# A third set of one-hots and a second pick ahead of the transposed weights, in layers 1 and 2 of a graph network

## The chip, the cores and the metric

The kernel runs on one core of a Trainium2 chip. The metric is the device time of one execution in microseconds (us), lower is better. The engines are called as the profile calls them: PE (the matrix engine), PEld (its weight loads), DVE (vector engine), ACT (scalar engine), POOL and SP (which here issues most of the DMA transfers).

## The reference

Three graph layers over 6250 nodes of 64 features and 206,250 edges sorted by target node (100,000 random pairs in both directions, and a loop at every node). One layer, cut to what matters:

```python
q, k, v = x @ Wq + bq, x @ Wk + bk, x @ Wv + bv
e = edge_attr @ We
alpha = sum(q[dst] * (k[src] + e), -1) / sqrt(64)
p = exp(alpha - segment_max(alpha, dst)[dst])
w = p / segment_sum(p, dst)[dst]
out = segment_sum((v[src] + e) * w[:, None], dst) + x @ Ws + bs
```

Layers 0 and 1 end with a relu and a layer norm; behind the last come a log-softmax, a residual and a final layer norm.

## The kernel before

Edges go in chunks of 512, four chunks to a unit (L513): some 102 units. A layer is a loop over rounds, one unit a round, 99 of them (`for u in range(NU - 3)`, L1862). Everything is unrolled at build time, so each engine has one fixed queue of instructions, in the order in which the Python code emits them.

**Source rows.** The features of the source nodes come in part from gathers by POOL (L601, released one at a time by a small copy to a `gate` tile, L635) and in part from *picks* on PE. A pick takes rows out of a table of node features held in SBUF (`halves`) by multiplying with one-hot matrices. The class `Picker` (L1280) plans them: the nodes are cut into pairs of windows, 11 pairs in layers 1 and 2, and one job covers one pair for four rounds, with the jobs staggered. So in four rounds 11 jobs are due, three in each of three rounds and two in the fourth. A job takes these steps:

- `load` (L1298): SP loads the keys of its edges into a `key` tile (L1307), of which there are seven.
- `aim` (L1319): DVE compares the keys with row numbers and so writes four one-hot tiles `hot` (L1331). A set is the four tiles of a job. Two sets exist, from two pools taken in turn. At most two finished sets may be outstanding (the guard ahead of `pop`).
- `bank` (L1356): 24 matmuls (L1374) into a PSUM tile of tag "x"; ACT copies the result to `kept` (L1383, or L1386 for the last pair); then comes the `aim` of the next job that has none.

The tag "x" has two PSUM buffers, so a third bank writes over the first one's. [...]

**A round in layers 1 and 2** (L1868 to L1890), in the order of emission:

1. `store` (last round's sums go to DRAM) and `close_up`, which moves the finishing of ended node groups one step on: normalisation, exponentials, projections, spread over several rounds (L1480 on).
2. `scores`: PE multiplies (L1673, L1678), DVE takes the maximum of each row (L1685) and its negative (L1687), ACT takes the exponentials into `prob` (L1692).
3. `naturals`: PE transposes of the picked rows of the next unit (L1399, L1404), copied by DVE (L1400, L1406) and ACT (L1407, L1409).
4. `bank`: the first pick that is due.
5. `turn`: gates of the gathers, and PE transposes of the gathered rows (L1650) with two copies by ACT (L1653).
6. `ask` and `across`: SP loads for the next unit (L1598, L1612, L1629). In the code these stand between the two calls of `turn`.
7. `weights`: PE transposes of `prob` (L1704), copied by DVE to `probT` (L1707).
8. `bank` for every other pick that is due.
9. `sums`: 32 matmuls with `probT` as the weights (L1717), copied by ACT (L1725); copies of `settle` (L618); another `aim`, if the guard lets it.

So the order on PE in a round with three picks is scores, naturals, pick, turn, weights, pick, pick, sums. Layer 0 has a loop body of its own and its own rules for picks.

Of the kernel before, what the change touches and what calls it, by code (L numbers as in the profile page):

```python
# [11 lines left out]
BF16 = mybir.dt.bfloat16  # L12
# [7 lines left out]
P = 128  # L20
# [12 lines left out]
LB = 4  # L33
FB = 4
BW = 4
SL = 16
# [6 lines left out]
TURN = 4  # L43
# [399 lines left out]
def main_path(  # L443
# [80 lines left out]
    picks = ctx.enter_context(tc.tile_pool(name="picks", bufs=3))  # L524
# [755 lines left out]
    class Picker:  # L1280
# [38 lines left out]
        def aim(self):  # L1319

            self.load()
            if not self.aims or self.aims[0] not in self.keys or len(self.hots) > (self.layer > 0):
                return
            job = self.aims.pop(0)
            a, b = self.span(job)
            pool = later if self.layer and self.aimed % 2 else picks
            self.aimed += 1
            made = []
            for h in range(BW):
                hot = pool.tile([P, TURN * LB, 2, SL], BF16, name="hot", bufs=BW)  # L1330
                nc.vector.tensor_scalar(  # L1331
                    hot[:, a:b].rearrange("p k w e -> p (k w e)"),
                    self.keys[job][:, a * 2 * SL : b * 2 * SL],
                    rank[:, h : h + 1],
                    None,
                    ALU.is_equal,
                )
                made.append(hot)
            self.hots[job] = made
            del self.keys[job]  # L1340
            self.load()

        def due(self, k):

            if not self.jobs or self.jobs[0][0] > k:
                return False
            return self.layer > 0 or k >= U0 or self.jobs[0] in self.hots

# [444 lines left out]
    def move(n):  # L1793

        for _ in range(n):
            next(sorting, None)
            serve()
# [36 lines left out]
    def step(n=1):  # L1834
        for _ in range(n):
            advance()

    def close_up(n=1):
        step(n)
        for _ in range(n):  # L1840
            advance(ending)
# [4 lines left out]
    for layer in range(L):  # L1846
        line = Line(layer)
        def free(u, j):
            lead = 2 * LB if not layer else min(2 * LB, LB + u)
            release(layer, u * LB + j + 1 + lead, nc.scalar.copy)  # L1850

        def drip(u, n=1):
            points[0] += n
            lead = 2 * LB if not layer else min(2 * LB, LB + u)
            most = LB * (T - 1) if not layer else LB + 1
            release(layer, u * LB + min(points[0], most) * LB / most + lead, nc.scalar.copy)
            if not layer:
                next(first_ranks, None)

        if not layer:  # L1860
            picker = Picker(layer)
        for u in range(NU - 3):  # L1862
            close = u >= CLOSE
            this = chunks[layer, u]
            points = [0]
            line.store()
            if waiting:
                active.append(waiting.pop(0))  # L1868
            if layer:
                close_up()  # L1870
                line.scores(u)
                drip(u)
                picker.naturals(u + 1, "ma")
                picker.bank(u + 2)
                close_up(3) if close else step()
                this.turn(0, lambda: drip(u, 0.5))
                ask(layer, u + 1)
                chunks[layer, u + 1].across()
                this.turn(1, lambda: drip(u, 0.5))
                close_up() if close else step()  # L1880
                line.weights(u)
                close_up(3) if close else step()
                while picker.due(u + 2):
                    picker.bank(u + 2)
                drip(u)
                picker.load()
                line.sums(u)
                free(u, LB - 1)
                settle(layer, u + 1)
                picker.aim()  # L1890
                continue
            paces = (2,) * 4 if u < 2 else (2, 1, 1, 1) if u < U0 + 1 else (1,) * 4
            line.weights(u - 1)
            close_up()
            this.turn(0, lambda: drip(u))
            close_up(3) if close else step()
            move(paces[0])
            drip(u, 2)
            line.sums(u - 1)
            drip(u)  # L1900
            move(paces[1])
            line.scores(u, exps=False)
            picker.naturals(u + 1, "p")
            if picker.due(u + 2):
                picker.bank(u + 2, "g")
            picker.aim()
            drip(u)
            ask(layer, u + 1)
            chunks[layer, u + 1].across()
            close_up() if close else step()  # L1910
            this.turn(1, lambda: drip(u))
            if u:
                chunks[layer, u - 1].exps()
            drip(u)
            close_up(3) if close else step()
            move(paces[2])
            while picker.due(u + 2):
                picker.bank(u + 2, "g")
            drip(u)
            picker.load()  # L1920
            move(paces[3])
            free(u, LB - 1)
            picker.aim()

        more = layer + 1 < L
        for _ in sorting:
            pass
        serve()
        if not layer:
            first_layer.close()  # L1930
            later = ctx.enter_context(tc.tile_pool(name="later", bufs=1))
            halves[1] = later.tile([P, NB - EARLY, 2, D], F32, name="halves1")
            kept[1] = later.tile([P, TURN * LB, D], F32, name="kept1")
            nc.vector.memset(kept[1][D:, :, PART - D :], 0.0)
        assert not picker.jobs
        if more:
            picker = Picker(layer + 1)
            picker.aim()
        def early(n=1):
            halve(layer + 1, n)  # L1940
            if more and picker.ready(0):
                picker.bank(0, "s")

        u = NU - 3
        line.weights(u - 1)
        line.sums(u - 1)
        line.scores(u)
        ask(layer, u + 1)
        chunks[layer, u + 1].across()
        full, rest = chunks[layer, u], chunks[layer, u + 1]  # L1950
        line.store()
        full.turn(0)
        free(u, 0)
        free(u, 1)
        close_up()
        line.weights(u)
        early(3)
        close_up()
        full.turn(1)
        free(u, 2)  # L1960
        free(u, 3)
        assert not pending
        line.scores(u + 1, "x")
        early(3)
        ask(layer, u + 2)
        last = chunks[layer, u + 2]
        last.across()
        line.sums(u)
        line.store()
        close_up()  # L1970
        rest.turn(0)
        early(2)
        line.weights(u + 1)
        close_up()
        line.scores(u + 2, "x")
        early()
        line.sums(u + 1)
        line.store()
        close_up()
        last.turn(0)  # L1980
        early()
        line.weights(u + 2)
        line.scores(u + 3, "m")
        early()
        close_up()
        line.sums(u + 2)
        line.store()
        close_up()
        early()
        line.weights(u + 3)  # L1990
        line.sums(u + 3)
        line.store()
        close_up()
        early()
        if more:
            ask(layer + 1, 0)
            chunks[layer + 1, 0].across()
        while active or len(ending) > 1:
            close_up()
            early()  # L2000
        while ending and (not more or (layer, groups[-1][0]) not in written):
            close_up()
            early()
        if more:
            assert all((layer, g) in written for g, n in groups)
            for k in range(FB):
                if (layer + 1, k) not in loaded:
                    fetch(layer + 1, k)
                if k:
                    await_turn(layer + 1, k)  # L2010
                else:
                    gather_all(layer + 1, k)
            while ending:
                close_up()
            halve(layer + 1, len(groups))
            while picker.due(0):
                picker.bank(0)
            picker.naturals(0, "ma")
            settle(layer + 1, 0)
            while picker.due(1):  # L2020
                picker.bank(1)
            picker.aim()
# [45 lines left out]
```

## Time and profile before

| | us |
|---|---|
| median of 3 runs | 4270.91 |
| lowest and highest | 4266.38, 4275.15 |
| the profiled execution, its time | 4275.86 |
| the profiled execution, its span | 4274.1 |

Layer 0 with the planning takes to about 1950 us, the rounds of layer 1 lie between about 2071 and 3035 us, those of layer 2 between about 3165 and 4195 us; between them and behind the last come the changes of layer. In the lists of waits a line names the engine, the tile and line that waited, then the engine, tile and line that it waited for, and then the time in total, how often, and the longest. "issue" means that nothing in the trace explains the gap, "remote" a release by something other than an engine's instruction. In the timeline the columns are the start in us, the duration, the engine, the line, the operation, the tiles written and read with their shapes, and the number of instructions taken together (x24), whose duration is from the first one's start to the last one's end; in brackets stands the idle time before it and what ended it. In the table of windows each stretch has its length, the busy time of PE, PEld, DVE, ACT and POOL with the number of instructions, the granted PE clock as a share of full speed, the busy share of the DMA engines and GB/s.

### The profile page before, as it was taken

Reading aid. Unit: us, or ns where it says so; the run is one execution under the profiler, and the core shown is the slowest. Engines: PE = TensorE matmul, PEld = TensorE weight load, DVE = VectorE, ACT = ScalarE, POOL = GpSimd, SP = SyncE. Lnnn points to the kernel's source line nnn. Section 1 sums busy time; section 2 is a strip of 40 time slices with the busy share of each in tenths; the row PEclk is TensorE's granted clock in tenths of the full one; section 3 lists DMA queues with packets and bytes.
Section 4 is the critical chain, followed back from the end, with each engine's and each line's share of the span. In section 5 each row is a group of like instructions: output and inputs, shape, how many; then the busy total and the mean of one; then the engine's idle time right before and its main releaser. Section 6 shows DMA issues by size and latency. Waiting matters only on the chain.

```text
span 4274.1 us, 125157 instructions
## 1 busy us (share of the span) xinstructions
PE 3681.7 (86%) x44542; PEld 2464.7 (58%) x44542; DVE 2891.1 (68%) x9241; ACT 2394.9 (56%) x7113; POOL 2067.3 (48%) x1910
## 2 busy tenths in 40 slices
PE   4679998889999999987889999998778998888885
PEld 2345555555555655654666666666456666666663
DVE  5566888787788777774566666666456666666664
ACT  2334555555555555543566666666536676666664
POOL 4454554555455665552444444444415444444442
PEclk9789999999999999997999999999879999999997
DMA  5447787787777888874677777777647777777773
GB/s 119 101 131 188 201 213 203 192 211 200 206 198 211 226 212 209 218 196 131 146 183 189 192 185 186 188 193 182 152 96 191 177 181 184 187 186 179 176 187 83
DMA packets 828647, 768.02 MB, mean 180 GB/s; under 512 B 393233, under 2 KB 628903, under 8 KB 828014
## 3 DMA queue, kind: packets, MB, share of 16 engines
q1 hardware_dynamic: 673282, 571.05, 54.2%
q10 hardware_dynamic: 93932, 126.48, 8.4%
q0 software_dynamic: 60800, 62.38, 7.8%
q8 instruction: 356, 5.83, 0.6%
q14 instruction: 277, 2.27, 0.2%
HBM read 599.30 MB, written 160.27 MB: 178 GB/s over the span
## 4 chain that ended last, share of the span: by engine, by line


## 5 line engine op out<-in xcount | busy, mean ns | idle before, releaser
L601 POOL DMA_INDIRECT feat<-in_x,gate x860 | 1050.6, 1222 | 884.4 <-ACT gate L635 686.4
L1331 DVE TENSOR_SCALAR hot<-key,rank 128x512 bf16<-128x512 f16 (+3 forms) x3024 | 908.2, 350 | 372.5 <-PE ps_x L1374 167.5
L601 POOL DMA_INDIRECT feat<-x,gate x816 | 796.8, 976 | 745.3 <-ACT gate L635 479.1
L1374 PEld LDWEIGHTS <-halves 128*64 128x64 bf16 x18144 | 963.4, 113 | 285.7 <-issue 206.1
L1374 PE MATMUL ps_x<-hot,halves 128*64 128x256 bf16 (+1 forms) x13248 | 836.7, 276 | 41.6 <-issue 31.2
L1717 PE MATMUL ps_g<-feat,probT 128*32 128x128 f32 x9672 | 436.5, 283 | 92.4 <-issue 61.6
L1064 PE MATMUL ps_x<-hit,rest 128*64 128x512 bf16 (+3 forms) x3200 | 459.1, 359 | 6.0 <-issue 5.1
L1409 ACT COPY featT<-kept 64x512 f32<-64x512 f32 x584 | 361.5, 619 | 144.3 <-PE ps_g L1374 42.6
L1053 DVE TENSOR_SCALAR hit<-ruler,pos 128x512 bf16<-128x512 f16 (+3 forms) x1600 | 422.9, 334 | 1.7 <-PE ps_m L1078 1.4
L1717 PEld LDWEIGHTS ps_g<-feat,probT 128*32 128x32 f32 x9672 | 286.5, 112 | 221.5 <-issue 175.6
L1685 DVE TENSOR_REDUCE most<-ps_s 128x1 f32<-128x512 f32 x297 | 204.1, 687 | 300.6 <-PE ps_s L1678 111.9
L601 POOL DMA_INDIRECT few<-x,gate x198 | 193.6, 978 | 379.4 <-ACT gate L635 113.0
L1374 PE MATMUL ps_g<-hot,halves 128*64 128x256 bf16 (+2 forms) x4560 | 302.3, 281 | 74.1 <-ACT kept L1383 28.5
L1653 ACT COPY featT<-ps_a 64x512 f32<-64x512 f32 x584 | 338.6, 580 | 15.6 <-PE ps_a L1650 4.1
L1678 PE MATMUL ps_s<-featT,q 128*32 128x512 f32 x2376 | 333.7, 621 | 2.9 <-ACT featT L1653 1.3
L1064 PE MATMUL ps_x<-hit,raw 128*64 128x512 bf16 (+3 forms) x1600 | 311.0, 367 | 4.5 <-issue 4.1
L1383 ACT COPY kept<-ps_x 128x256 f32<-128x256 f32 (+2 forms) x502 | 185.1, 370 | 210.8 <-remote 128.6
L635 ACT COPY gate<-src_b 128x1 int32<-128x1 int32 x1762 | 289.9, 191 | 8.7 <-ACT keys L1136 1.4
L1692 ACT ACTIVATE prob<-ps_s,part 128x512 f32<-128x512 f32 x297 | 204.2, 688 | 161.0 <-issue 48.7
L1704 PE MATMUL ps_p<-ident,prob 128*128 128x128 f32 (+1 forms) x1224 | 199.1, 286 | 91.9 <-ACT prob L1692 89.8
L1064 PEld LDWEIGHTS <-rest 128*64 128x64 bf16 x3200 | 203.8, 113 | 116.6 <-issue 30.0
L1725 ACT COPY part<-ps_g 128x128 f32<-128x128 f32 (+1 forms) x309 | 82.2, 266 | 273.0 <-PE ps_g L1717 43.8
(261 smaller groups left out, 5162.4 us busy)
## 6 DMA issues: line engine op xcount, KB each, us to landing
feat<-eaP SPq DMA_DIRECT2D x292, 512.0 KB
featT<-eaS SPq DMA_DIRECT2D x292, 512.0 KB
key<-keyS SPq DMA_DIRECT2D x712, 128.0 KB
raw<-in_ea SPq DMA_DIRECT2D x200, 256.0 KB
eaS<-eT ACTq DMA_DIRECT2D x200, 256.0 KB
eaP<-eN ACTq DMA_DIRECT2D x200, 256.0 KB
to<-toS SPq DMA_DIRECT2D x292, 128.0 KB
part<-part SPq DMA_DIRECT2D x600, 32.5 KB
```

The source lines that it names most:

```text
L601: nc.gpsimd.indirect_dma_start(out=spares[layer, k] if c is None else loaded[layer, k][:, c, t, 0], out_offset=None, in_=xts[layer][:, :], ...
L635: copy(gate, index[:, i : i + 1])
L1053: nc.vector.tensor_scalar(hit, ruler[:, : REACH[t]], self.pos[:, at : at + 1], None, ALU.is_equal)
L1064: nc.tensor.matmul(self.px[i][j * D : (j + 1) * D, : REACH[t]], self.part(i, part)[:, (j * T + t) * D : (j * T + t + 1) * D], self.hits[t, ...
L1331: nc.vector.tensor_scalar(hot[:, a:b].rearrange("p k w e -> p (k w e)"), self.keys[job][:, a * 2 * SL : b * 2 * SL], rank[:, h : h + 1], None,
L1374: nc.tensor.matmul(px[w * D : (w + 1) * D, a:b], third(halves[block >= EARLY][:, at : at + 1], part)[:, 0], made[h][:, a:b, w], start=(h = ...
L1409: nc.scalar.copy(featT[:D, :, w * P : (w + 1) * P], kept[0][w * D : (w + 1) * D, at : at + LB])
L1653: nc.scalar.copy(self.featT[:D, :, at : at + P], pt[h * D : (h + 1) * D])
L1678: nc.tensor.matmul(self.p_s[rows], self.q[:, j * STRIDE : j * STRIDE + W], self.featT[:, j, :], start=False, stop=True)
L1685: nc.vector.tensor_reduce(top[:n], self.p_s[:n], AX.X, ALU.max)
L1692: nc.scalar.activation(self.prob[:n], self.p_s[:n], AF.Exp, bias=self.part[:n, P : P + 1], accum_out=self.part[:n, P + 1 : P + 2],)
L1717: nc.tensor.matmul(p_g[rows, :].rearrange("n (h d) -> n h d", h=2), self.probT[:, t, rows], batch[:, c + j, t], start=(t == 0), stop=(t == ...
```

## The change

The one-hots of layers 1 and 2 get a third set: of three jobs one takes the tiles of pool `picks` (four tiles, one set) and two take those of pool `later` (eight tiles, two sets, 4 KB a partition more). The one-hots of a job thus overwrite those of the job three before it, not two. The guard in `aim` stays: at most two finished sets are outstanding. `due` can look past the first job, and when two more jobs are due behind the first pick, a second call of `bank` stands right behind the first. In a round with three picks the order becomes scores, naturals, pick, pick, turn, weights, pick, sums. A round with two picks keeps its order.

```diff
             job = self.aims.pop(0)
             a, b = self.span(job)
-            pool = later if self.layer and self.aimed % 2 else picks
+            pool, sets = (later, 2) if self.layer and self.aimed % 3 else (picks, 1)
             self.aimed += 1
             made = []
             for h in range(BW):
-                hot = pool.tile([P, TURN * LB, 2, SL], BF16, name="hot", bufs=BW)
+                hot = pool.tile([P, TURN * LB, 2, SL], BF16, name="hot", bufs=BW * sets)
                 nc.vector.tensor_scalar(
...
-        def due(self, k):
+        def due(self, k, behind=0):
 
-            if not self.jobs or self.jobs[0][0] > k:
+            if len(self.jobs) <= behind or self.jobs[behind][0] > k:
                 return False
             return self.layer > 0 or k >= U0 or self.jobs[0] in self.hots
...
                 picker.bank(u + 2)
+                if picker.due(u + 2, 1):
+                    picker.bank(u + 2)
                 close_up(3) if close else step()
```

## The prediction

> **What bounds the kernel now.** I read the page first, for the busy shares, then the windows of the two layers that the change touches (the 99 rounds of layer 1, about 2071 to 3035 us, and of layer 2, about 3165 to 4195 us), then what ended the idle time of each engine there, and last the timeline of PE, DVE and ACT in single rounds.
>
> ```profile
> PE 3681.7 (86%) x44542; PEld 2464.7 (58%) x44542; DVE 2891.1 (68%) x9241; ACT 2394.9 (56%) x7113; POOL 2067.3 (48%) x1910
> ...
> 2071.00:3035.00 964.00, 880.42 (x11700) 621.89 (x11692) 625.02 (x1831) 629.21 (x1917) 454.10 (x467) 0.99 0.76 186
> 3165.00:4195.00 1030.00, 915.85 (x12158) 646.45 (x12155) 658.96 (x1977) 687.19 (x2050) 481.48 (x490) 0.98 0.74 180
> ```
>
> In both layers PE is busy for 91% and 89% of the time (880.42 of 964.00, 915.85 of 1030.00), DVE and ACT for about 65% each. So PE's order is the path: a change is worth what it takes out of PE's idle time (84 and 114 us), and DVE and ACT count only where PE waits for them. PE's waits, layer 1 first, then layer 2:
>
> ```profile
> PE ps_g L1717 <- issue: 29.5, 89, 1.1
> PE ps_p L1704 <- ACT prob L1692: 13.8, 23, 0.9
> PE ps_g L1717 <- DVE probT L1707: 1.9, 5, 0.5
> ```
> ```profile
> PE ps_p L1704 <- ACT prob L1692: 41.0, 35, 3.4
> PE ps_g L1717 <- issue: 22.2, 68, 1.0
> PE ps_x L1374 <- ACT kept L1383: 4.5, 12, 0.9
> PE ps_g L1717 <- DVE probT L1707: 3.6, 8, 0.5
> ```
>
> Two things stand out. The transposes of the weights (L1704) wait for ACT's exponentials, 54.8 us over both layers in 58 waits; this is the wait that the moved bank stands in front of. And the sums (L1717) have small gaps, 51.7 us in 157, for which the trace names no releaser. A round with three picks and the one with two that follows it, on PE:
>
> ```profile
> 2511.10 0.60 PE L1704 MATMUL ps_p<-ident,prob 128*128 128x128 f32 x4
> 2511.63 2.81 PE L1374 MATMUL ps_x<-hot,halves 128*64 128x256 bf16 x48
> 2514.37 1.09 PE L1717 MATMUL ps_g<-feat,probT 128*32 128x128 f32 x23
> 2515.75 0.50 PE L1717 MATMUL ps_g<-feat,probT 128*32 128x128 f32 x9 [0.29 <-issue]
> 2516.18 0.39 PE L1673 MATMUL ps_s<-to,codeT 128*128 128x512 bf16 x1
> ...
> 2520.45 0.60 PE L1704 MATMUL ps_p<-ident,prob 128*128 128x128 f32 x4
> 2520.98 1.50 PE L1374 MATMUL ps_x<-hot,halves 128*64 128x256 bf16 x24
> 2522.48 1.08 PE L1717 MATMUL ps_g<-feat,probT 128*32 128x128 f32 x32
> 2523.49 0.39 PE L1673 MATMUL ps_s<-to,codeT 128*128 128x512 bf16 x1
> ```
>
> I call the picks of a round B1, B2 and B3: 24 matmuls each, some 1.4 us each (2.81 for two). Here nothing waits for prob. The sums take 2516.18 - 2514.37 = 1.81 us behind two banks and 2523.49 - 2522.48 = 1.01 us behind one.
>
> **The change part by part.** *The moved bank.* In three of every four rounds of layers 1 and 2, so in about 148 of 198, B2 goes ahead of turn (L1650) and weights (L1704). PE has the same instructions; in a clean round like the one above their sum and the next round's start are unchanged. What is gained must come from the 58 waits for prob. B2 has no wait of its own: its one-hots were made in the round before, its PSUM buffer was read by ACT then. So B2's 1.4 us fill the wait at L1704. The question is what is late next. Here is a round that waits, PE first, then ACT:
>
> ```profile
> 2552.43 0.66 PE L1704 MATMUL ps_p<-ident,prob 128*128 128x128 f32 x4 [0.84 <-ACT prob L1692]
> 2553.02 3.04 PE L1374 MATMUL ps_x<-hot,halves 128*64 128x256 bf16 x48
> ```
> ```profile
> 2551.60 0.69 ACT L1692 ACTIVATE prob<-ps_s,part 128x512 f32<-128x512 f32 x1
> ...
> 2552.48 0.36 ACT L1407 COPY feat<-ps_a 32x256 f32<-32x256 f32 x1
> 2552.85 1.25 ACT L1409 COPY featT<-kept 64x512 f32<-64x512 f32 x2
> 2554.13 0.37 ACT L1383 COPY kept<-ps_x 128x256 f32<-128x256 f32 x1
> ```
>
> The tag "x" has two PSUM buffers, so B3 writes the buffer of B1 and must wait until ACT has copied B1 out (kept, L1383). That copy stands on ACT behind the exponentials, a gate and the copies of L1407 and L1409; it ends at 2554.13 + 0.37 = 2554.50, which is 2.2 us after the exponentials. B3's own 24 take 1.50, so they began at about 2553.02 + 3.04 - 1.50 = 2554.56: 0.06 us after the copy. That is why the two banks together took 3.04 and not 2.81. With B2 moved ahead, PE does B2 in the wait, then the weights, and B3 stands alone behind the weights: it still cannot begin before 2554.50, because nothing ahead of that copy on ACT has moved. The sums begin when they did. So in such a round the 0.84 us leave L1704 and come back as a wait of L1374 for kept; the gain is 0.0. The clean round has the same neighbourhood: its copy of B1, with the row
>
> ```profile
> 2512.09 0.37 ACT L1383 COPY kept<-ps_x 128x256 f32<-128x256 f32 x1
> ```
>
> ends at 2512.46, and B3 began there at about 2511.63 + 2.81 - 1.50 = 2512.94. Only 0.5 us are left to win before this copy binds.
>
> It is otherwise where the wait is so long that PE's clock falls, in layer 2:
>
> ```profile
> 3784.77 0.66 PE L1704 MATMUL ps_p<-ident,prob 128*128 128x128 f32 x4 [3.37 <-ACT prob L1692]
> 3785.36 4.48 PE L1374 MATMUL ps_x<-hot,halves 128*64 128x256 bf16 x48
> 3789.76 1.08 PE L1717 MATMUL ps_g<-feat,probT 128*32 128x128 f32 x32
> ```
> ```profile
> 3786.47 0.37 ACT L1383 COPY kept<-ps_x 128x256 f32<-128x256 f32 x1
> ```
>
> Behind 3.37 us of idleness the 48 matmuls take 4.48 us instead of 2.81. Moved ahead, B2 leaves about 1.9 us of that wait; B3 can begin at 3786.84 and the sums 1.50 later at 3788.4 at full clock, or 2.24 later (half of 4.48) at 3789.1. That is 0.7 to 1.4 us earlier than 3789.76. [...]
>
> How many are there? In layer 1 a wait for prob has 13.8/23 = 0.6 us in the mean. If layer 2's ordinary ones are like that, 35 x 0.6 = 21.0 of its 41.0 us are ordinary, and the other 20.0 come from 20.0/(3.4 - 0.6) = 7 long ones. Gain: 7 x (0.7 to 1.4) = 5 to 10 us; I take 7. For the other 51 waits the bounds are 0 (the copy binds at once, as at 2554.50) and all they hold, 54.8 - 7 x 3.4 = 31 us, if the copy were always early. I take 0, by the row that I have.
>
> *One-hots on DVE ahead of probT.* Each bank ends with making four one-hots for the pick after next. So eight, not four, now stand on DVE ahead of the copy of the transposed weights (probT, L1707), for which the sums wait; and that copy is covered by one bank on PE instead of two.
>
> ```profile
> 2510.32 1.29 DVE L1331 TENSOR_SCALAR hot<-key,rank 128x512 bf16<-128x512 f16 x4
> 2511.73 0.69 DVE L1707 COPY probT<-ps_p 128x512 f32<-128x512 f32 x1
> ```
>
> In the clean round the eight would run from 2510.32 to about 2512.8; the weights, 1.4 us later than now, end at about 2513.1; probT runs to 2513.8; the sums begin at 2514.4 as now. DVE keeps about 0.3 us of room ahead of probT and PE 0.5 behind it: 0.8 us in all. This tail, one bank between weights and sums, is that of the rounds with two picks, and the trace has its price: if all 1.9 + 3.6 = 5.5 us of waits for probT were theirs, it is 5.5/50 = 0.11 us a round, or 16 us for 148. The lower bound is 0. I take 1, since the clean round still has room; 16 stays for the range.
>
> *The third set.* Before, the one-hots of a pick overwrite those of the pick whose matmuls are just running, so DVE waits for PE. Layer 1, then layer 2:
>
> ```profile
> DVE hot L1331 <- PE ps_x L1374: 83.3, 99, 2.6
> ```
> ```profile
> DVE hot L1331 <- PE ps_x L1374: 77.1, 129, 2.1
> ```
>
> With three sets this 160 us mostly goes. It lies beside PE's work: PE waited for probT for 5.5 us, and no line of its waits names one-hots. The guard that allows at most two finished sets is not changed, so no one-hots are made further ahead. I cost it at nothing; without it the moved bank's second set of four would have to wait for B1's and B2's matmuls ahead of probT, so the set pays for the order.
>
> *Queues that B2 is moved past.* On ACT its copy (0.37 us) now stands ahead of the gates and of the featT copies of turn, which are first used in the next round; nothing on PE's path. On SP the next key load stands ahead of the loads for the next unit. These are wanted a round (9 us) later; I cost both at 0.
>
> Sum against the profiled execution (4275.86 us, span 4274.1 and 1.8 around it): -7 + 1 = -6, so 4270. It was 5 us above the median of the runs, 4270.9; from the median the forecast is 4265.
>
> **The rivals.** *A: the slow sums are cured.* Behind 48 matmuls the sums take 0.80 us longer than behind 24. If the cause is the uninterrupted run of two banks into the sums, the new order, which has the tail of a round with two picks, ends it: 0.80 x 148 = 118 us, with the 6 above 4147; half of it gives 4206. For it: the gaps at L1717 without a releaser, 157 times. [...]
>
> *B: probT comes late (slower).* In a round in which the finishing of a node group puts work on DVE ahead of the one-hots, the room of 0.8 us is used up. Its largest instruction there, in layer 1:
>
> ```profile
> L1505 DVE TENSOR_TENSOR both<-both,mm x10: 1209/1218/1220, 2171.4 to 2952.2; 128x1024 f32<-128x1024 f32 x10
> ```
>
> One of its 1.21 us makes the sums wait 0.4 us, two of them 1.6. Ten groups end in a layer, about 87 us or nine rounds apart (2952.2 - 2171.4 over 9), and the steps of one spread over several rounds; with two three-pick rounds of each group hit, 40 rounds lose 16 to 64 us. It decides as soon as DVE is over 0.8 us behind. For it: eight one-hots in front. Against: the 5.5 us that the same tail costs now. With the 16 us above and no more than the 6 gained, 4281; the low ones of its cases meet the forecast.
>
> *C: nothing moves.* The long waits also return at L1374 (the slower featT copies and the second copy, ahead of the gates, shift what follows), and the time stays at 4271 within a few us.
>
> **How the numbers follow.** Forecast (waits move to the copy of B1, only the long ones pay): 0.55, from 4255 to 4270, the likeliest 4265. A: 0.16. B: 0.21. C: 0.08. A measurement of this kernel can tell about 0.2%, 8.5 us, from no change. Faster by more: all of A and not quite half of the forecast, 0.16 + 0.25 = 0.41. Slower by more: B without its mildest, 0.20. The same: the rest, 0.39. The range goes from half of A, 4205, to the upper part of B, 4288; full A (half of its chance, 0.08) and the worst of B (0.06) are left out.
>
> **What would show it.** Right: the waits of L1704 for prob fall from 54.8 us to a few, those of L1374 for kept L1383 rise from layer 2's 4.5 to some 45 in both (54.8 less what pays); in clean rounds the next codeT matmul still comes 9.3 us after the last; DVE's waits for ps_x at L1331 nearly vanish without a change of PE's time; the half-clock banks behind the long waits go. Wrong: the sums take 1.0 us in rounds with three picks too (A), or L1717's waits for probT go beyond 15 us (B), or L1704's waits go and no other wait of PE grows, which would mean that the copy of B1 did not bind.

## The result and the profile after

The changed kernel is slower: 4332.76 us (median of 4, 4329.89 to 4335.36) against 4270.77 us, 62 us between the medians; the ratio is put at 1.0129 (95% interval 1.0104 to 1.0154), some 55 us. The forecast was 4265, the range 4205 to 4288. On two other chips the same two kernels gave 1.0133 (1.0088 to 1.0178) and 1.0063 (1.0037 to 1.009); the chips come up below.

The windows of the two layers after, over nearly all of their rounds, with the columns as before:

```profile
2083.00:3062.00 979.00, 880.40 (x11508) 628.81 (x11502) 599.86 (x1807) 616.55 (x1896) 473.07 (x461) 0.96 0.75 182
3256.00:4260.00 1004.00, 869.58 (x11554) 618.88 (x11553) 614.95 (x1895) 653.65 (x1958) 477.94 (x466) 0.97 0.73 177
```

The same rounds before:

```profile
2081.00:3035.00 954.00, 871.75 (x11592) 615.78 (x11584) 619.93 (x1818) 623.97 (x1902) 449.19 (x462) 0.99 0.76 186
3225.00:4206.00 981.00, 871.00 (x11577) 613.20 (x11566) 628.96 (x1899) 658.67 (x1958) 458.40 (x466) 0.97 0.75 181
```

Both layers lost: 25 us (979 against 954) and 23 us (1004 against 981). PE is busy for about as long (7 us more, and a lower granted clock in layer 1, 0.96 against 0.99), so most of it is idle time of PE. What PE waited for, from the first round of layer 1 to the last of layer 2, before:

```profile
PE ps_p L1704 <- ACT prob L1692: 70.2, 60, 14.9
PE ps_g L1717 <- issue: 53.8, 162, 1.1
...
PE ps_g L1532 <- ACT part L1725: 23.5, 23, 3.6
PE ps_g L1717 <- DVE probT L1707: 12.7, 16, 6.0
...
PE ps_g L1446 <- ACT part L1725: 7.2, 10, 3.3
PE ps_x L1374 <- ACT kept L1383: 6.2, 18, 0.9
```

and after:

```profile
PE ps_x L1374 <- ACT kept L1383: 53.1, 48, 1.7
PE ps_g L1717 <- issue: 44.8, 123, 1.6
PE ps_p L1704 <- ACT prob L1692: 41.5, 24, 14.9
PE ps_x L1374 <- issue: 37.8, 73, 1.4
PE ps_g L1532 <- ACT part L1725: 37.6, 23, 3.6
PE ps_g L1446 <- ACT part L1725: 18.4, 10, 3.3
...
PE ps_g L1717 <- DVE probT L1707: 7.2, 4, 5.6
```

The 14.9 us in both lists is one wait between the layers. The wait did move as forecast, from prob at L1704 to kept at L1374. But it grew on the way: L1704 fell by 29 us and L1374's wait for kept rose by 47. And two waits that the forecast did not name grew by 25 us together: the projections of the finishing (L1532, L1446), which need the PSUM tile of the sums and so ACT's copy of it (part, L1725). DVE's waits for PE at L1331 went, as forecast. The one-hots on the page, before and then after:

```profile
L1331 DVE TENSOR_SCALAR hot<-key,rank 128x512 bf16<-128x512 f16 (+3 forms) x3024 | 908.2, 350 | 372.5 <-PE ps_x L1374 167.5
```
```profile
L1331 DVE TENSOR_SCALAR hot<-key,rank 128x512 bf16<-128x512 f16 (+3 forms) x3024 | 871.0, 350 | 88.3 <-DMA key<-keyS 23.8
```

How the projections came to wait shows in one round near 2290 us, the same in both programs. Before, PE and then ACT:

```profile
2288.88 0.27 PE L1717 MATMUL ps_g<-feat,probT 128*32 128x128 f32 x1 [0.34 <-issue]
2289.54 1.10 PE L1532 MATMUL ps_g<-ve,wT 128*128 128x64 f32 x8 [0.40 <-ACT part L1725]
```
```profile
2289.22 0.27 ACT L1725 COPY part<-ps_g 128x128 f32<-128x128 f32 x1
```

After, PE and then ACT:

```profile
2288.10 0.38 PE L1717 MATMUL ps_g<-feat,probT 128*32 128x128 f32 x2 [0.26 <-issue]
2290.85 1.86 PE L1532 MATMUL ps_g<-ve,wT 128*128 128x64 f32 x8 [2.37 <-ACT part L1725]
```
```profile
2288.13 0.37 ACT L1383 COPY kept<-ps_x 128x256 f32<-128x256 f32 x1 [1.20 <-PE ps_x L1374]
2288.40 0.19 ACT L635 COPY gate<-src_b 128x1 int32<-128x1 int32 x1
2290.53 0.27 ACT L1725 COPY part<-ps_g 128x128 f32<-128x128 f32 x1 [1.94 <-remote]
```

After, the sums end at 2288.48 and ACT is free from 2288.59, with nothing to do but copy them; it begins at 2290.53. Before, the copy began 0.07 us after the sums. So the news that the sums are done reached ACT 1.94 us late. It was late on PE's side: the trace's record of the semaphore that the copy waits for, which PE alone updates, has the update at 2290.51, 0.02 us before the copy starts. (The profile models the ends of matmuls, so it does not tell whether the matmul ended late or only its signal came late.) I call this a late completion, and counted the waits that one ended in the timelines of layers 1 and 2: for each maximum (L1685), each copy of probT and each copy part, but not for the copies to kept, the time from the end of PE's last instruction for it, or of the instruction ahead on its own engine if that is later, to its start, where PE was the later of the two and the time is over 0.6 us. Ordinarily it is 0.04 to 0.07 us.

| kernel | waits ended by a late completion | us late in all |
|---|---|---|
| before | 44 | 86 |
| changed | 69 | 124 |

### The profile page after: what moved, and what is told of

Its sections match the earlier page's. It is cut to its first block, busy times and chain, and to the rows that moved or that the text cites. A ratio compares the mean times of both kernels' runs of the same rounds, so it can differ in the third digit from the quotient of the medians.

```text
span 4328.2 us, 124259 instructions
## 1 busy us (share of the span) xinstructions
PE 3689.9 (85%) x44542; PEld 2483.8 (57%) x44542; DVE 2858.8 (66%) x9241; ACT 2387.6 (55%) x7113; POOL 2105.2 (49%) x1910
## 4 chain that ended last, share of the span: by engine, by line
## 5 line engine op out<-in xcount | busy, mean ns | idle before, releaser
L1374 PEld LDWEIGHTS <-halves 128*64 128x64 bf16 x18144 | 973.2, 113 | 333.1 <-issue 264.2
L1331 DVE TENSOR_SCALAR hot<-key,rank 128x512 bf16<-128x512 f16 (+3 forms) x3024 | 871.0, 350 | 88.3 <-DMA key<-keyS 23.8
L1374 PE MATMUL ps_x<-hot,halves 128*64 128x256 bf16 (+1 forms) x13248 | 830.4, 276 | 101.9 <-ACT kept L1383 54.0
L1685 DVE TENSOR_REDUCE most<-ps_s 128x1 f32<-128x512 f32 x297 | 204.4, 688 | 511.3 <-PE ps_s L1678 283.9
L1717 PE MATMUL ps_g<-feat,probT 128*32 128x128 f32 x9672 | 411.0, 285 | 81.9 <-issue 53.0
L1409 ACT COPY featT<-kept 64x512 f32<-64x512 f32 x584 | 361.2, 618 | 163.1 <-PE ps_g L1374 40.8
L601 POOL DMA_INDIRECT few<-x,gate x198 | 235.2, 1188 | 409.5 <-ACT gate L635 91.7
L1717 PEld LDWEIGHTS ps_g<-feat,probT 128*32 128x32 f32 x9672 | 282.1, 113 | 183.6 <-issue 123.4
L1678 PE MATMUL ps_s<-featT,q 128*32 128x512 f32 x2376 | 369.8, 638 | 4.2 <-ACT featT L1653 1.2
L1374 PE MATMUL ps_g<-hot,halves 128*64 128x256 bf16 (+2 forms) x4560 | 307.0, 284 | 69.1 <-ACT kept L1383 26.8
L1383 ACT COPY kept<-ps_x 128x256 f32<-128x256 f32 (+2 forms) x502 | 172.8, 371 | 198.6 <-PE ps_x L1374 108.3
L1725 ACT COPY part<-ps_g 128x128 f32<-128x128 f32 (+1 forms) x309 | 82.2, 266 | 336.2 <-remote 84.0
L1704 PE MATMUL ps_p<-ident,prob 128*128 128x128 f32 (+1 forms) x1224 | 196.2, 284 | 61.3 <-ACT prob L1692 60.6
```

Source lines behind the costliest of these rows:

```text
L601: nc.gpsimd.indirect_dma_start(out=spares[layer, k] if c is None else loaded[layer, k][:, c, t, 0], out_offset=None, in_=xts[layer][:, :], ...
L1331: nc.vector.tensor_scalar(hot[:, a:b].rearrange("p k w e -> p (k w e)"), self.keys[job][:, a * 2 * SL : b * 2 * SL], rank[:, h : h + 1], None,
L1374: nc.tensor.matmul(px[w * D : (w + 1) * D, a:b], third(halves[block >= EARLY][:, at : at + 1], part)[:, 0], made[h][:, a:b, w], start=(h = ...
L1409: nc.scalar.copy(featT[:D, :, w * P : (w + 1) * P], kept[0][w * D : (w + 1) * D, at : at + LB])
L1678: nc.tensor.matmul(self.p_s[rows], self.q[:, j * STRIDE : j * STRIDE + W], self.featT[:, j, :], start=False, stop=True)
L1685: nc.vector.tensor_reduce(top[:n], self.p_s[:n], AX.X, ALU.max)
```

## The experiments

The runs came from several chips, and these are of two kinds. On four occasions (the first profiles' among them) the kernel before takes 4271 to 4320 us and has late completions; on two chips it takes 3826 and 3830 us and none of the eight kernels profiled there has a single wait in this count; the kernel before is not among the eight. Every ratio is against the kernel before on the same chip. In the expectations, theory G is the gate that I saw in the prediction (the third bank waits for ACT's copy of the first pick), L and S hold that late completions make the loss (S: because PE's queue runs ahead without a hold), D that it lies in DVE or DMA, F that it comes with instruction fetches or the mere place of instructions.

### The parts alone, and the gate taken away

The third set alone (`sets_only`): the first two hunks of the change, the order left.

> The third set of one-hots with the old order on PE. If the loss comes from the order (moved bank), this stays within 0.3% of before: 4259 to 4283 us, while DVE's waits for ps_x at L1331 (160 us in layers 1 and 2) mostly vanish. If the loss comes from DVE being ahead (key loads and aims earlier, in the way of others), most of the 62 us appear here: 4310 or more.

The order alone (`order_only`): the other two hunks, two sets.

> The moved bank with two sets. If the order alone makes the loss, this is at least as slow as the changed kernel, 4325 to 4350 us: probT now also stands behind one-hots that wait for the matmuls of the second bank. If the third set makes the loss, it is near before, 4260 to 4285.

The gate taken away, in the changed kernel (`changed_third_in_m`) and in the one before (`before_third_in_m`):

```diff
                 if picker.due(u + 2, 1):
                     picker.bank(u + 2)
+                    third_pick = "m"
+                else:
+                    third_pick = "x"
...
-                    picker.bank(u + 2)
+                    picker.bank(u + 2, third_pick)
```

(In the kernel before, the second pass of the loop behind the weights, so again the third pick, gets the tag m.)

> The changed kernel, but the third pick of a round writes the PSUM tag m and not x, so it no longer waits for ACT's copy of the first pick. Theory G (that copy is the gate, and the new order leaves the third bank alone in front of it): the waits of L1374 for kept L1383 (52 us in both layers) vanish and the time falls by 40 us or more, to 4290 or below. Theory L (PE's completions reach ACT and DVE late, at places that the order sets; the gate is a symptom): the waits for kept vanish too but return at L1532, L1446, L1717 or as issue, and the time stays above 4315.

> The kernel before, with its third pick in tag m. Theory G: the third bank started 0.05 us after the copy in more than half of the rounds with three picks, so the sums now begin earlier in those; 10 to 40 us faster, 4230 to 4260. Theory L: within 0.3% of before, since what is won ahead of the sums is lost again where the completions come late.

| kernel | median us | ratio to 4277.83 (interval) | late completions, us |
|---|---|---|---|
| sets_only | 4313.17 | 1.009 (1.0059 to 1.012) | 109, 230 |
| order_only | 4344.73 | 1.0149 (1.0095 to 1.0202) | 48, 94 |
| changed_third_in_m | 4319.63 | 1.0115 (1.0068 to 1.0162) | 83, 161 |
| before_third_in_m | 4292.02 | 1.004 (1.0011 to 1.0069) | 74, 141 |

Two surprises. The third set alone, which puts not one instruction of PE elsewhere, costs 0.9%, most of the loss. And a third pick that need not wait gains nothing: it made the kernel before slower, and left the changed one within its interval. So G, as the whole story, fell. What the three that loosen a wait have in common is lateness (230, 161 and 141 us; the kernel before was not profiled on this chip, its 86 us are those of the first profile). In `sets_only` PE's waits are:

```profile
PE ps_p L1704 <- ACT prob L1692: 94.7, 80, 14.9
PE ps_x L1374 <- issue: 51.1, 99, 1.3
PE ps_g L1532 <- ACT part L1725: 40.3, 23, 3.7
```

against 70.2, 28.3 and 23.5 in the first profile: prob and part come later, though the engines that make them have no more to do. The order alone is different: it has little lateness and is the slowest. With two sets the second bank's one-hots stand ahead of probT and wait for PE's matmuls, which I forecast to be what the third set is for. DVE does wait 202.3 us for ps_x there, but PE's wait for probT is no larger for it (12.0 us, 12.7 in the first profile); PE waits for kept, 55.9 us. So what the order alone loses by is not shown. Each edit alone loses about as much as both together (1.0129): the two losses do not add.

### Holding PE's queue

If completions come late when PE's queue runs on with nothing to stop it, a wait in the right place should bring them in time. The kernels `..._held` have a 1x1 matmul ahead of the first pick that reads DVE's negative maximum of the round; `sets_placebo` has one that reads a constant.

```diff
+            if held is not None:
+                nc.tensor.matmul(px[:1, a, :1], held, held, start=True, stop=True)
...
-                picker.bank(u + 2)
+                picker.bank(u + 2, held=chunks[layer, u - 1].part[:, P : P + 1] if u else None)
```

> The third set with the old order, and ahead of the first pick of each round one tiny matmul (1x1) that reads DVE's negative maximum of the round (L1687), so PE's queue is held there until the scores are through DVE. Theory S (PE's completions come late when its sequencer runs far ahead with a full queue, and DVE's waits for PE used to hold it back): lateness of the scores' completions (75 us in the third-set kernel for the maximum alone, 237 in all) falls by half or more and the time falls by 20 to 50 us against the third set alone, to 4265 to 4295. Rival F (lateness goes with instruction fetches alone) or D (DVE and DMA are in each other's way): the holding only costs PE time, some 0.1 us in 198 rounds: 4325 to 4340.

> The same tiny matmul in the third-set kernel, but it reads a constant and waits for nothing. All theories: within 12 us of the third set alone, 4300 to 4325, with its lateness unchanged. If it is faster by over 20 us, a mere shift of PE's instructions does it (rival F).

> The changed kernel with the holding matmul. Theory S: 4333 falls by 15 to 45 us, to 4288 to 4318, since the scores' completions come at once; the rest of its loss, at the sums' copy, stays. Rivals F and D: 4345 or more.

> The kernel before with the holding matmul. Theory S: it has only 52 us of lateness at the maximum to lose and pays some 20 us for the holding: 4245 to 4285, about the same. Rivals F and D: 4290 or more.

These four fell on a chip without late completions, where the kernel before takes 3826.35 us. Ratios: `sets_held` 1.0117 (1.0083 to 1.0152), `sets_placebo` 1.0052 (1.0035 to 1.0069), `changed_held` 1.0159 (1.0142 to 1.0176), `before_held` 1.0146 (1.0124 to 1.0168). No lateness in any, so they say nothing for or against S; they price the hold, at over 1%. What they show besides is how PE runs when nothing is late. Two banks and the sums behind them, in the placebo:

```profile
2259.48 2.81 PE L1376 MATMUL ps_x<-hot,halves 128*64 128x256 bf16 x48
2262.22 1.08 PE L1719 MATMUL ps_g<-feat,probT 128*32 128x128 f32 x32
```

The sums that took 1.8 us behind two banks in the first profile take 1.0 here (2262.22 to the next matmul at 2263.23), with no gap, and so they do in the two other whole rounds with two banks ahead of the sums between 2250 and 2290 us. In the first profile of the kernel before they take, from the first one's start to the last one's end, 2.17 us in the median of the rounds with three picks and 1.08 in that of the rounds with two.

So three were run again, and the kernel before for its profile:

> The changed kernel unaltered, since the last four kernels ran on a chip on which the kernel before takes 3826 us and no completion of PE came more than 0.6 us late. If this chip is of that kind: theory S says that the change then has no cost, 3810 to 3835 (within 0.3% of before, by the copy of the first pick, as forecast); a loss that lies in DVE or DMA (D) would be there too, 1% or more, 3860 and up. If the chip is of the kind with late completions (before 4270 to 4280): 1.0 to 1.5% slower, 4315 to 4340, by both.

> The third set alone. On a chip without late completions: S says within 0.2% of before (DVE's waits for PE were off the path), D says 0.5% slower or more. On one with them: 0.7 to 1.2% slower by both.

> The third set with the holding matmul. On a chip without late completions it costs again about 1.2% (0.25 us in 198 rounds), which tells nothing of S. On one with late completions: S says that the lateness falls by half or more and that the time is below that of the third set alone, by 20 us or more less the 50 us that the holding cost on the other chip, so between 30 us below and 30 us above it; the lateness decides, not the time. F says that the lateness stays at about 230 us.

> The kernel before, for its profile on this chip. On a chip of the second kind no completion comes more than 0.6 us late (none did in four kernels) and the sums take 1.1 us in rounds with three picks too. On one of the first kind: 86 us of lateness, as in the first profile.

| kernel | median us | ratio to 4320.03 (interval) | late completions, us |
|---|---|---|---|
| before_again (one run) | 4318.22 | | 33, 67 |
| changed_again | 4376.02 | 1.0133 (1.0088 to 1.0178) | 72, 130 |
| sets_again | 4378.72 | 1.011 (1.0052 to 1.0167) | 119, 266 |
| sets_held_again | 4348.68 | 1.0049 (1.0027 to 1.0072) | 52, 103 |

This chip has late completions, and the numbers of the first come back. As it has profiles of the kernel before, of the set alone and of the whole change, it also tells where the time goes. The table has means over the 144 rounds with three picks, in us from the start of a round's first matmul of the scores (L1673):

| | before_again | sets_again | changed_again | sets_held_again |
|---|---|---|---|---|
| scores end on PE | 1.49 | 1.53 | 1.76 | 1.59 |
| DVE's maximum begins | 2.28 | 2.82 | 2.60 | 2.24 |
| exponentials begin | 3.64 | 4.17 | 3.99 | 3.60 |
| the copy of the first pick ends | 6.93 | 7.41 | 7.20 | 6.73 |
| sums begin | 8.68 | 9.31 | 9.09 | 8.99 |
| the next round begins | 11.22 | 11.55 | 11.57 | 11.31 |

With the set alone the scores end when they did, and the maximum begins 0.54 us later. DVE is not what holds it back: from the later of the scores' end and of DVE's own last instruction to the maximum it stands idle for 0.85 us in the mean of all rounds, against 0.33 before (0.03 in the placebo, on the chip without lateness). The exponentials, the copy of the first pick and the sums follow, and the round is 0.33 us longer. The moved bank on top of the set makes it no longer (11.55 and 11.57), and the medians of the two kernels, 4378.72 and 4376.02 us, agree. So with the set in place the move costs nothing that can be told from noise. DVE's waits in layers 1 and 2, in `before_again` and then in `sets_again`, show them moving from the one-hots, which are gone from the head of the second list, to the maximum:

```profile
DVE hot L1331 <- PE ps_x L1374: 166.1, 221, 2.6
DVE most L1685 <- PE ps_s L1678: 80.6, 63, 4.5
```
```profile
DVE most L1685 <- PE ps_s L1678: 156.7, 74, 7.2
DVE most L1685 <- remote: 117.9, 31, 5.9
DVE most L1685 <- PE ps_a L1404: 102.4, 32, 5.6
```

The hold, which costs over 1% where nothing is late, here cuts lateness from 266 to 103 us and the median by 30 us. The two intervals overlap a little, so the gain is likely rather than certain; the fall in lateness is plain, and the maximum begins as early as before. That speaks for S and against F.

The count above is of waits, and so it changes with who waits. The record of PE's semaphore gives another, of its signals, whether an engine waited or not: of some 1830 groups of matmuls in the two layers, those whose signal came over 0.6 us after the modelled end of the last matmul are 546 (901 us in all) in `before_again`, 672 (1288) in `sets_again`, 623 (1236) in `changed_again` and 565 (990) in `sets_held_again`; in the placebo, on the other kind of chip, 31. By this measure too lateness rises with the set and falls with the hold, but by 43% in time and not fourfold: most late signals are there in the kernel before as well, at places where fewer of them end a wait for a maximum, probT or part.

A cheaper hold reads the maximum (L1685, kept as `top`) and not its negative (`..._held_max`). The changed kernel ran once more beside these:

```diff
-                picker.bank(u + 2, held=chunks[layer, u - 1].part[:, P : P + 1] if u else None)
+                picker.bank(u + 2, held=chunks[layer, u - 1].top if u else None)
```

> The third set with the old order, the first pick of a round held by a 1x1 matmul that reads DVE's maximum (L1685) and not its negative: the hold ends about 0.25 us earlier, when PE has just done the work ahead. Theory S, on a chip with late completions: lateness 80 to 130 us as with the other hold, and 30 us or more faster than the third set alone, so at most 0.4% slower than before, perhaps faster. On a chip without: 0 to 0.5% slower than before. F or D: 1% slower than before on any chip.

> The kernel before with that hold. S, with late completions (67 to 86 us of lateness before): lateness at the maximum halves, the hold costs some 10 us: between 0.5% faster and the same. Without late completions: 0.1 to 0.5% slower. F or D: 0.3% slower or more on any chip.

> The changed kernel with that hold. S, with late completions: lateness at the maximum (61 to 76 us) halves, 15 to 40 us faster than the changed kernel, 0.4 to 1.0% slower than before. If the order has no cost but through lateness, it comes out at sets_held_max within 0.3%; if it has one (the wait for the copy of the first pick, PE's idling at L1532), it stays 0.5% or more above it.

> The changed kernel beside these. With late completions: 1.0 to 1.5% slower than before. Without: S says within 0.3% of before, D says 1% slower or more.

Again a chip without lateness (before 3830.15 us): `sets_held_max` 1.0066 (1.004 to 1.0092), `before_held_max` 1.007 (1.0048 to 1.0092), `changed_held_max` 1.0114 (1.0082 to 1.0145), `changed_third` 1.0063 (1.0037 to 1.009). With the same hold the third set costs nothing here (1.0066 against 1.007, and 1.0117 against 1.0146 with the first hold): its 0.9 to 1.1% were seen only where completions come late. Without a hold the set did not run here; the placebo's 0.5% is no more than its own matmul would cost (an estimate: its first pick starts 2.46 us into a round, in the median, and that of `changed_third` 2.34, so 0.12 us in 198 rounds, 24 us). The changed order costs 0.4 to 0.5% on top of the same set and hold (1.0159 against 1.0117, 1.0114 against 1.0066, the intervals just overlapping), and the whole change 0.6%. So my S was wrong in expecting no loss at all here, D was wrong in expecting 1% or more of the change, and the 0.7% of `before_held_max` is what F or D had said and not S (0.1 to 0.5%). PE's waits in layers 1 and 2 of `changed_third`:

```profile
PE ps_x L1374 <- ACT kept L1383: 46.7, 38, 1.7
PE ps_p L1704 <- ACT prob L1692: 34.6, 32, 7.2
PE ps_x L1374 <- DVE hot L1331: 12.5, 9, 1.8
```

and of the placebo, which has the old order and the third set (its lines are two further down), for the same stretch:

```profile
PE ps_p L1706 <- ACT prob L1694: 60.2, 60, 6.6
...
PE ps_x L1376 <- ACT kept L1385: 4.5, 17, 0.9
```

The order moves 26 us out of prob, puts 42 into kept and 12.5 into one-hots that the second pick now wants earlier: 29 us more in all. But these waits are not lost time: the rounds with three picks, where the order acts, take 9.53 us in the changed kernel and 9.54 in the placebo (means of 144), and the sums begin after 8.07 and 8.10 us. Nor do the held pairs show such a cost in the two layers, which from the first maximum to the last are 6 and 7 us longer with the new order (1837 against 1832 us, 1853 against 1846), while the medians differ by 13 and 9. So G is not shown for the order's own cost. What makes the changed kernel 25 us slower than the one before here (3855.02 against 3830.15) stays open, as the kernel before has no profile on a chip of this kind.

### The gate moved, not removed

ACT's 1.25 us of copies at L1409 stand between the exponentials and the copy of the first pick. They can go ahead of the exponentials, as soon as the scores have left their buffer:

```diff
-                line.scores(u)
+                scored = line.scored
+                line.scores(u, exps=False)
+                picker.copies(u + 1)
+                for v in range(scored, line.scored):
+                    chunks[layer, v].exps()
                 drip(u)
-                picker.naturals(u + 1, "ma")
+                picker.naturals(u + 1, "ma", early=True)
```

(`copies` has the two copies of L1409, taken out of `naturals`.)

> The changed kernel with ACT's copies of L1409 behind the scores and ahead of the exponentials, so the copy of the first pick comes some 1 us sooner after the exponentials, which themselves start about 0.25 us later. Theory G for the order's own cost: the waits of L1374 for kept (47 to 57 us) fall to 15 or less, and the kernel gains 10 to 30 us on the changed one: 0.2% faster to 0.4% slower than before without late completions, 0.5 to 1.0% slower with them. If the cost of the order lies elsewhere (one-hots of the second pick not ready, ACT's later copies), the waits fall and the time does not: 0.6% slower and 1.3% slower.

> The kernel before with the same move. The weights wait for the exponentials there with nothing ahead of them, so the later start costs and the nearer copy gains: between 0.3% faster and 0.3% slower than before without late completions, 0 to 0.5% slower with them (taking the gate away by tag m made it 0.4% slower).

On a chip with late completions (before 4279.72 us) `changed_copies_first` took 4236.29 us, a ratio of 0.9911 (0.9879 to 0.9943): it beats both kernels, where I had forecast a loss of 0.5 to 1.0%. `before_copies_first` took 4284.62, 1.0012 (0.9992 to 1.0031): no difference. PE's waits in the faster one (L1712 is its weights, L1725 its sums, L1540 and L1454 its projections):

```profile
PE ps_g L1725 <- issue: 94.9, 237, 1.1
PE ps_p L1712 <- ACT prob L1700: 49.9, 37, 15.4
...
PE ps_g L1540 <- ACT part L1733: 13.3, 23, 3.3
...
PE ps_x L1374 <- ACT kept L1383: 4.6, 18, 0.9
PE ps_g L1454 <- ACT part L1733: 4.5, 10, 0.8
```

The wait for kept is gone (4.6 us), prob costs 49.9 (15.4 of it between the layers), and the projections wait 18 us and not 56. One of its rounds on ACT, and the third bank on PE:

```profile
2493.65 1.25 ACT L1417 COPY featT<-kept 64x512 f32<-64x512 f32 x2
2494.92 0.69 ACT L1700 ACTIVATE prob<-ps_s,part 128x512 f32<-128x512 f32 x1
...
2496.24 0.37 ACT L1383 COPY kept<-ps_x 128x256 f32<-128x256 f32 x1
```
```profile
2497.67 0.60 PE L1712 MATMUL ps_p<-ident,prob 128*128 128x128 f32 x4
2498.20 1.50 PE L1374 MATMUL ps_x<-hot,halves 128*64 128x256 bf16 x24
```

The copy of the first pick ends at 2496.61, 1.6 us before the third bank starts (0.5 us in the clean round before). The exponentials end at 2495.61, 2.1 us ahead of the weights. This is the room that the moved bank makes: it lets the exponentials start later. It exists only in rounds with three picks, and the two kinds of round show it, in mean us from one L1673 to the next (`before` and the changed kernel are from the first profiles, the others from this chip):

| rounds | before | changed | before_copies_first | changed_copies_first |
|---|---|---|---|---|
| 144 with three picks | 11.12 | 11.42 | 10.87 | 10.46 |
| 50 with two | 8.88 | 9.00 | 9.96 | 10.15 |

The rounds with two picks, where no bank was moved, lose over 1 us with the early copies in either kernel: their sums take 2.5 us from the first to the last and not 1.25. That gives back some 57 of the 138 us won in the others (estimates against the changed kernel: 50 x 1.15 and 144 x 0.96). Why these sums become slow is open, and a kernel that moves the copies in rounds with three picks alone was not run.

Lateness does not explain the gain. At the maximum, probT and part it is the lowest here, 22 waits and 46 us (45 and 67 in `before_copies_first`), but the copies to kept, which that count leaves out, add some 165 waits and 300 us by the same rule, more than in any other kernel (before 37 and 53, changed 80 and 124). So lateness moved to a copy that here has some 1.5 us of room (the median of the rounds with three picks).

## Why the prediction was wrong

**The third set.** The step "I cost it at nothing" failed. It was right that DVE's 160 us of waits were off the path and that they would go; wrong that nothing else changes with them. On chips with late completions the set alone costs 0.9 and 1.1% (35 and 59 us between the medians), against 1.3% for the whole change, and on one of them the way is plain: the news that the scores are done reaches DVE later, the maximum begins 0.54 us later, the sums 0.63, and the round is 0.33 us longer. That late completions are the link is shown as far as this: they rise with the set (on one chip from 67 to 266 us as counted, and from 901 to 1288 us over all of PE's groups), the set costs nothing under the same hold on the chips that have none, and a hold on PE's queue cuts them and, most likely, the time. Why PE's completions come late at all, and why more so with a third set, is not settled. Nor does any run show what sets the two kinds of chips apart. The amount of lateness is no full account either: `before_third_in_m` has 141 us of it and lost only 0.4%, and the fastest kernel has as much as any once kept is counted.

**The moved bank.** The wait went where the forecast put it, from prob to the copy of B1. That kept rose by more than prob fell, 47 against 29 us, is no cost of the move: the set alone had raised prob (70.2 us in the first profile, 94.7 in `sets_only`), and from the set to the whole change, on one chip, the rounds stay as long (11.55 and 11.57 us). Against the kernel before, "The sums begin when they did" failed, by 0.41 us a round there, but they begin 0.63 us later with the set alone; on top of the set the zero held. With two sets the move alone lost 1.5%; the forecast gave it no number. The 5 to 10 us forecast from the long waits could not be seen apart from that, and their number was a guess from means: layer 2 had four of 3.4 us before, not seven, and the longest in its rounds afterwards is 2.3. That the banks at half clock behind them would go failed too: the granted clock was 0.50 behind one of the four before (3786 to 3788 us), and it was 0.50 in the changed kernel as well, behind 2.28 us for prob and 1.47 for kept (3830.5 to 3833.8 us), where the third bank took 2.76 us and not 1.50. The step that DVE has room for eight one-hots held: L1717's wait for probT fell from 12.7 to 7.2 us.

**The rivals.** A is out as a gain: in `changed_copies_first`, with one bank between weights and sums, the sums have 94.9 us of gaps, more than in any other, so two banks were not their only cause; and in the profile before, the sums behind the two banks of 4.48 us took 1.08 us. B had the right sign by the wrong mechanism; probT was not late. C had the waits return at L1374, as they did, but no loss. That the slower side had only B's 0.20 came from pricing DVE's waits as free.

## What to carry to other kernels

A wait off the path may still set when other engines meet. Here 160 us of such waits went with a third buffer, and the kernel lost 1% on one kind of chip. So a buffer that takes away idle time off the path is worth a run by itself, not a zero. When two edits make one change, run each alone on the same chip: here each lost alone, and the parts did not add up to the whole. And when work is moved into a wait, look for the wait that is next: here the move paid only after ACT's order was changed to match it, and then the two together gave 0.9%, where each alone gave a loss or nothing.

## What the runs showed of the hardware

The same program took 3826 and 3830 us on two chips and 4271 to 4320 us on the others, over 10% apart. On the faster ones sums ran at 1.08 us for 32 matmuls behind two banks (`sets_placebo`, at 2262 us) and no wait for a maximum, a copy of probT or a copy part was ended by a completion over 0.6 us late; on the slower ones up to 4.1 us lay between the modelled end of a matmul of the scores and the maximum that waited for it (the first profiles, before and changed). What a change is worth differed with the kind: the third set 0.9 to 1.1% against nothing (under a hold), the whole change 1.3% against 0.6%.
